# Two-layer convolution kernel: the sums of points 3 and 4 by accumulating DMA, the group norms' steps issued singly, and new instruction lists

## The chip, the cores and the metric

One Trainium2 chip, one core. The metric is device time in microseconds of one execution of the whole program; lower is better. PE is TensorE (matrix products), DVE is VectorE, ACT is ScalarE, POOL is GpSimd, SP is SyncE. SP and POOL do nothing here but issue DMAs, apart from POOL's preparations at the start. SBUF is the working memory, PSUM the memory that PE writes.

## The reference

The input is 16 images of 128 channels and 64x64 pixels, float32. Two residual layers follow each other, each behind a group norm with 32 groups of 4 channels.

```python
def _gn(v, G=32, eps=1e-5):
    g = v.reshape(B_, G, C_ // G, H_, W_)
    m = jnp.mean(g, axis=(2, 3, 4), keepdims=True)
    s = jnp.var(g, axis=(2, 3, 4), keepdims=True)
    return ((g - m) / jnp.sqrt(s + eps)).reshape(v.shape)

# layer 0: a 3x3 convolution as an analog crossbar would compute it
v = jnp.round(jnp.clip(x, -1.0, 1.0) * 127) / 127 * 0.6
fv = patches + 0.1 * patches ** 3              # patches: 3x3 windows of v, zeros around
g = g_pos - g_neg                              # 3 slices of 128x128x3x3
outs = [jnp.einsum('bctfyx,ocyx->btfo', fv, g[i]) for i in range(3)]
adc = lambda y: jnp.clip(jnp.round(y * 0.01 * 256) / 256, -16, 16)
mem_out = adc(outs[2]) + 4 * adc(outs[0]) + 2 * adc(outs[1]) + adc(outs[2])
x = x + mem_out * output_factor + bias

# layer 1: on tokens t = 4096 pixels, 128 -> 64 -> 128 channels
q, k, v = Wq @ xf, Wk @ xf, Wv @ xf
out = Wm @ (q * (exp(B) @ (exp(k) * v)) / (exp(B) @ exp(k)))
x = x + out
```

## The kernel before

**The convolution by points.** Rows are taken in 16 tiles of four. For each tile the kernel does not form the nine shifted products but evaluates the input at six points (0 to 5: the points 0, 1, -1, 2, -2 and infinity of a polynomial in the row), multiplies there with weights evaluated at the same points, and interpolates the four output rows back. Along a row, even and odd columns are combined into sums `cs`, differences `cq` and neighbour differences `cd`, so that a point's product is four matrix products with 512 columns. `weights` (from L286) evaluates the weights once at the start: `us[i]` holds four points of slice `i`, `ud[i]` points 0 and 5.

A *block* is one slice of weights for one image, so an image has three blocks. A block has two *halves*: `h = 0` handles points 1 and 2, `h = 1` points 3 and 4. Half `k` of an image (k = 0 to 5; block k // 2, half k % 2) is made of these operations, whose names stand in the lists below with `.k` behind:

- `q1u`, `q2u`, `q0u`, `q3u` (PE, u = 0 or 1 for the two points): the four products, into the PSUM tiles `pa` and `pb`. `m1u`, `sdu`, `sAu` (ACT) copy `pa` out between them, to `d`, negated to `pb`, and to `s`. A product that reads or continues what a copy needs waits for the copy.
- `Bo` (DVE, L588) makes the second column of the two points' results, in `s[:, :, 1]`; `df` (DVE, L589) takes the difference of the two points into `d`; `sm` (L593 on) puts their sum into `s[:, 1]`. Of the two halves, `h = 0` gets its sum by a DMA that POOL issues and that adds in flight (L597), and `h = 1` by a custom DVE operation that also doubles it (`doubled_sum`, L561).
- Half k of the next block carries the rest of the block before it: `ma` and `mc` (DVE, `middle`, L558: the two inner rows, bounded and rounded to int16; `ma` from the differences, `mc` from the sums of both halves), `S0` and `S3` (DVE, L615 and L618: sums and differences of both halves joined), `P`, `o0`, `o1` (PE: points 0 and 5), `bc` (ACT), `tk` (DVE: the two outer rows), and `aA`, `aB` (adding the block to the image's total: by POOL's DMA or, for the first slice, a doubling on DVE).

**The rest of an image.** `li`, `lj` load a quarter of the next image twice (SP), `sx` and `sy` sum and square it (ACT), `x0`, `xa`, `pmx`, `xb`, `pvx`, `xc`, `xl`, `xd` are its group norm: `x0` a shift, `xa` to `xd` groups of two to five DVE instructions on 128x1 or 128x2 values, `pm` and `pv` two matmuls, `xl` two ACT instructions. Then `n`, `cl`, `s`, `va` quantize, clip and cube it, and `gr`, `er`, `p0`, `p5`, `pa`, `pb`, `cs`, `cq`, `cd`, `e0`, `e5` (DVE) evaluate it at the points. After the convolution `cx` (ACT), `cd0x` to `cd3x` (POOL's accumulating DMA) and `sq` form the layer's output and its squares, `y0` to `yd` are the second group norm, and the second layer runs on four quarters or *pairs* p: `xn`, `kp`, `vp`, `qp`, `ek`, `ekv`, `dn`, `g`, `u`, `ln`, `ex`, `oa`, `ob`, `oc`, `op`, `r`, `rd` (POOL's accumulating DMA), `st` (SP's store).

**What sets the order.** Every engine executes its instructions in the order in which the program names them. That order is written out in lists of operation names. `ORDER` (L39) is one turn of the steady state, which runs for most images; `+1` behind a name means that in this turn the operation belongs to the image before. `FIRST` (L62) is the start with the first images, where `+2` is preparation: `hs`, `hq`, `hn`, `hc`, `hr`, `hv` stand for the sums, squares, quantization, clip, square and value of the four quarters of image 0, `hz`, `hcs`, `hcq`, `hcd` for its points 1 and 2, and `W0a` to `W2p` for steps of the three slices' weights (`a` negates the loaded weights on ACT, `A` is POOL's DMA that adds the positive ones). `LAST` (L95) is the end; there the last block's rest is `tma`, `tmc`, `tS0`, `tS1`, `tk0`, `tk3`, `tx` (joining into the output), `ts` (squares), its norm is `tsh` to `tnd`, and the last image's pairs are written with a capital (`Xn0`, `Kp0`). A wait is inserted wherever an operation needs what another engine or a DMA makes or still reads. A DMA is issued when its turn comes in the queue of the engine that issues it and its inputs are there.

Of the kernel before, what the change touches and what calls it, by code (L numbers as in the profile page):

```python
# [11 lines left out]
I32 = mybir.dt.int32  # L12
# [3 lines left out]
ALU = mybir.AluOpType  # L16
# [23 lines left out]
    cl0+1 q01.2+1 S3.2+1 q00.2+1 sq2+1 tk.2+1 cl1+1 cd0x+1 sA1.2+1 q31.2+1 q11.3+1 s0+1 sA0.2+1  # L40
    m11.3+1 va0+1 q30.2+1 s1+1 q21.3+1 q10.3+1 sq1+1 m10.3+1 P.3+1 q20.3+1 Bo.2+1 sd1.3+1 q01.3+1
    va1+1 df.2+1 lj2+1 sq3+1 lj3+1 gr0+1 sd0.3+1 st3+1 sq0+1 q31.3+1 q30.3+1 sA1.3+1 bc.3+1 q00.3+1
    ya+1 Bo.3+1 sA0.3+1 pmy+1 yb+1 o0.3+1 n2+1 pvy+1 er0+1 st2+1 n3+1 yc+1 o1.3+1 q10.4+1 yl+1 cl2+1
    yd+1 xn0+1 q11.4+1 sm.2+1 tk.3+1 df.3+1 kp0+1 cp+1 vp0+1 m11.4+1 P.4+1 cl3+1 ma.4+1 m10.4+1
    aB.3+1 q20.4+1 ek0+1 bc.4+1 s3+1 ekv0+1 sd0.4+1 dn0+1 sm.3+1 mc.4+1 va3+1 q21.4+1 s2+1 g0+1 li0
    sx0 xn1+1 li1 S0.4+1 u0+1 ln0+1 sd1.4+1 oa0+1 x0 o0.4+1 o1.4+1 q30.4+1 ex0+1 tk.4+1 vp1+1 ob0+1
    qp0+1 kp1+1 oc0+1 aA.2+1 op0+1 va2+1 ek1+1 r0+1 ekv1+1 gr1+1 q01.4+1 sx1 q31.4+1 q00.4+1 sA0.4+1
    P.5+1 S3.4+1 sA1.4+1 bc.5+1 q10.5+1 Bo.4+1 q11.5+1 rd0+1 df.4+1 m10.5+1 er1+1 dn1+1 sy0 g1+1
    u1+1 sm.4+1 o0.5+1 o1.5+1 oa1+1 m11.5+1 st0+1 q21.5+1 aA.4+1 ln1+1 q20.5+1 pa0+1 tk.5+1 ex1+1
    sd1.5+1 pb0+1 q01.5+1 ob1+1 sd0.5+1 q00.5+1 cq0+1 xn2 qp1+1 q30.5+1 q31.5+1 oc1+1 cd0+1 cs0+1  # L50
    Bo.5+1 op1+1 sA0.5+1 kp2 r1+1 li2 vp2 q10.0 ek2 sA1.5+1 P.0 bc.0 q11.0 ekv2 pa1+1 o0.0 m11.0
    m10.0 dn2 q21.0 df.5+1 q20.0 sm.5+1 sx2 o1.0 rd1+1 aB.5+1 sd1.0 pb1+1 mc.0 g2 S0.0 sd0.0 sy2 sy1
    ma.0 q01.0 u2 st1+1 oa2 q30.0 q31.0 ln2 tk.0 ex2 xn3 ob2 q00.0 li3 qp2 kp3 cq1+1 lj0 ek3 sA0.0
    oc2 cs1+1 op2 S3.0 vp3 Bo.0 sA1.0 q11.1 r2 P.1 bc.1 ekv3 df.0 dn3 o1.1 g3 aA.0 cd1+1 m11.1 rd2
    o0.1 sx3 u3 tk.1 q21.1 oa3 sy3 ln3 ex3 q10.1 sd1.1 qp3 m10.1 q20.1 ob3 sd0.1 oc3 op3 p5 sm.0 r3
    q01.1 aB.1 xa q00.1 pmx sA1.1 e5 p0 q30.1 xb sA0.1 e0 cx2 q31.1 cx1 pvx xc Bo.1 lj1 xl rd3 P.2
    bc.2 cx0 cd2x q10.2 q11.2 cd1x o1.2 m11.2 q21.2 df.1 sm.1 cx3 m10.2 xd q20.2 ma.2 o0.2 n0 cd3x
    sd1.2 mc.2 sd0.2 y0 S0.2 n1
# [4 lines left out]
    hs0+2 hs2+2 x0+2 hs3+2 hq0+2 hq2+2 hi+2 hq1+2 hs1+2 hq3+2 xa+2 pmx+2 xb+2 pvx+2 xc+2 xl+2 xd+2  # L63
    hn3+2 hn2+2 hc2+2 hn1+2 hn0+2 W2a+2 W1a+2 W0a+2 hc0+2 hc3+2 hc1+2 W0A+2 hr1+2 hr0+2 hv1+2 hv0+2
    gr0+2 W1A+2 er0+2 hr2+2 W0b+2 li0+1 hv2+2 W0j+2 cp+2 W0c+2 W0f+2 W0e+2 W0d+2 W0g+2 W0i+2 W0h+2
    hr3+2 li1+1 W0J+2 W0n+2 hv3+2 W0l+2 er1+2 sx0+1 W0m+2 W1c+2 x0+1 hz1+2 gr1+2 hcq1+2 W1b+2 pa1+2
    hcs1+2 hcd1+2 W2A+2 W1j+2 sx1+1 W0p+2 sy0+1 W0o+2 q10.0+1 sy1+1 li3+1 hz0+2 li2+1 W1e+2 W2b+2
    hcs0+2 W2c+2 m10.0+1 p0+1 sx3+1 pb1+2 q11.0+1 sx2+1 m11.0+1 q20.0+1 hcq0+2 W1f+2 q21.0+1 sy2+1
    cd1+2 sy3+1 hcd0+2 W1J+2 sd0.0+1 xa+1 sd1.0+1 q01.0+1 sA1.0+1 W1d+2 cs1+2 pmx+1 lj0+1 W2J+2
    q31.0+1 cq1+2 q00.0+1 q30.0+1 xb+1 pvx+1 q11.1+1 W1g+2 sA0.0+1 W1h+2 e0+1 Bo.0+1 m11.1+1 q10.1+1  # L70
    m10.1+1 W2d+2 W1i+2 W2e+2 q20.1+1 W1l+2 lj1+1 xc+1 W1m+2 W2g+2 sd0.1+1 df.0+1 q21.1+1 W2j+2 xl+1
    W0k+2 P.2+1 sm.0+1 sd1.1+1 q00.1+1 xd+1 W1n+2 q01.1+1 W1o+2 W2f+2 bc.2+1 sA0.1+1 p5+1 W2h+2
    q31.1+1 n0+1 q10.2+1 W1p+2 q30.1+1 sA1.1+1 W2i+2 cl0+1 Bo.1+1 m10.2+1 q20.2+1 W2m+2 sd0.2+1 n1+1
    o0.2+1 q11.2+1 W1k+2 q00.2+1 m11.2+1 df.1+1 sm.1+1 q30.2+1 q21.2+1 e5+1 ma.2+1 mc.2+1 S0.2+1
# [886 lines left out]
```

## Time and profile before

| | us |
|---|---|
| median of three runs | 1575.94 (1574.69 to 1576.45) |
| the profiled execution | 1571.91 |
| its span, first to last instruction | 1570.1 |
| mean granted PE clock over the span | 0.979 of full speed |

A line of a group or of the timeline gives: start (timeline only), duration, engine, line of the code, operation, tile written <- tiles read, shape, count; behind it in brackets the engine's idle time before it and who ended that. The DMA lines that matter here:

```profile
acc<-y POOLq DMA_DIRECT2D x62, 512.0 KB, 7.0
x<-in_x_dram POOLq DMA_DIRECT2D x60, 512.0 KB, 8.3
xn<-x POOLq DMA_DIRECT2D x58, 512.0 KB, 4.6
out_dram<-xn SPq DMA_DIRECT2D x58, 512.0 KB, 5.3
s<-s POOLq DMA_DIRECT2D x48, 512.0 KB, 5.6
```

The last number is the median time from issue to landing. `s<-s` is the sum `sm` of the halves `h = 0`, one for each of 48 blocks. In the 92 us of a steady image the DMA engines are busy 66% of the time.

### The profile page before, as it was taken

Reading aid. Unit: us, or ns where it says so; the run is one execution under the profiler, and the core shown is the slowest. Engines: PE = TensorE matmul, PEld = TensorE weight load, DVE = VectorE, ACT = ScalarE, POOL = GpSimd, SP = SyncE. Lnnn points to the kernel's source line nnn. Section 1 sums busy time; section 2 is a strip of 40 time slices with the busy share of each in tenths; the row PEclk is TensorE's granted clock in tenths of the full one; section 3 lists DMA queues with packets and bytes.
Section 4 is the critical chain, followed back from the end, with each engine's and each line's share of the span. In section 5 each row is a group of like instructions: output and inputs, shape, how many; then the busy total and the mean of one; then the engine's idle time right before and its main releaser. Section 6 shows DMA issues by size and latency. Waiting matters only on the chain.

```text
span 1570.1 us, 14797 instructions
## 1 busy us (share of the span) xinstructions
PE 1481.1 (94%) x4684; PEld 564.2 (36%) x4684; DVE 1427.7 (91%) x1817; ACT 1115.6 (71%) x1859; POOL 223.1 (14%) x254
## 2 busy tenths in 40 slices
PE   1589999999999999999999999999999999999996
PEld 0233333333333433333343333433333333333331
DVE  4999999999999999999999999999999999998774
ACT  4655868687686868768686776968678686865654
POOL 2001011120201112011121201112020111201120
PEclk6799999999999999999999999999999999999997
DMA  6226478484756848476593847759385774835375
GB/s 175 78 70 132 111 165 195 107 183 134 153 147 153 209 90 181 138 155 161 131 208 98 174 137 164 173 115 219 96 168 141 165 183 108 195 87 121 81 128 154
DMA packets 67359, 227.01 MB, mean 145 GB/s; under 512 B 7632, under 2 KB 8272, under 8 KB 67280
## 3 DMA queue, kind: packets, MB, share of 16 engines
q0 software_dynamic: 38480, 125.52, 43.2%
q1 hardware_dynamic: 28512, 99.50, 18.4%
q10 hardware_dynamic: 288, 1.05, 0.2%
q8 instruction: 37, 0.61, 0.2%
q14 instruction: 42, 0.34, 0.1%
HBM read 102.30 MB, written 33.55 MB: 87 GB/s over the span
## 4 chain that ended last, share of the span: by engine, by line
PE 51%; DVE 28%; ACT 10%; issue 6%; DMA 5%; DVEq 0%; POOL 0%; ACTq 0%; POOLq 0%
PE py L551 15%; PE pa L551 14%; PE pb L551 7%; PE pz L745 5%; DVE y L558 5%; PE py L767 4%; DVE d L589 3%; DVE acc L558 3%; ACT gs L359 3%; PE py L745 3%; DVE s L615 3%; PE pz L755 2%; DMA x<-in_x_dram 2%; DVE f L502 2%; DVE s L561 2%
## 5 line engine op out<-in xcount | busy, mean ns | idle before, releaser
L551 PE MATMUL py<-v,ud 128*128 128x512 f32 x760 | 363.1, 610 | 0.0
L551 PE MATMUL pa<-cs,us 128*128 128x512 f32 x384 | 195.1, 611 | 34.2 <-DVE us L327 33.1
L551 PE MATMUL pb<-cd,us 128*128 128x512 f32 x384 | 192.7, 609 | 12.4 <-ACT pb L582 10.5
L551 PE MATMUL pa<-cq,us 128*128 128x512 f32 x384 | 197.1, 616 | 4.1 <-ACT d L580 3.9
L551 PEld LDWEIGHTS py<-v,ud 128*128 128x128 f32 x760 | 137.5, 189 | 170.4 <-issue 149.3
L551 PE MATMUL pa<-cd,us 128*128 128x512 f32 x384 | 194.6, 609 | 3.6 <-DVE x L363 2.5
L582 ACT ACTIVATE pb<-pa 128x512 f32<-128x512 f32 x192 | 112.4, 585 | 66.6 <-PE pa L551 61.6
L580 ACT ACTIVATE d<-pa 128x512 f32<-128x512 f32 x192 | 110.8, 594 | 44.1 <-PE pa L551 31.0
L808 POOL DMA_DIRECT2D xn<-x x58 | 50.2, 870 | 607.5 <-ACT xn L778 600.3
L585 ACT ACTIVATE s<-pa 128x512 f32<-128x512 f32 x192 | 111.0, 594 | 35.6 <-PE pa L551 29.8
L588 DVE SCALAR_TENSOR_TENSOR s<-d,pb 128x1024 f32<-128x1024 f32 x96 | 116.6, 1215 | 5.7 <-PE pb L551 5.6
L589 DVE TENSOR_TENSOR d<-s 128x1024 f32<-128x1024 f32 x96 | 117.1, 1220 | 2.9
L551 PEld LDWEIGHTS pa<-cs,us 128*128 128x128 f32 x384 | 68.3, 190 | 140.0 <-issue 53.4
L745 PE MATMUL pz<-xn,w 128*64 128x512 f32 x464 | 117.0, 604 | 0.0
L778 ACT ACTIVATE xn<-py,scalars 128x512 f32<-128x512 f32 x116 | 73.7, 690 | 59.9 <-PE py L767 59.9
L551 PEld LDWEIGHTS pb<-cd,us 128*128 128x128 f32 x384 | 68.3, 190 | 112.0 <-issue 71.0
L640 POOL DMA_DIRECT2D acc<-y x62 | 72.6, 1170 | 250.8 <-DVE y L558 221.1
L551 PEld LDWEIGHTS pa<-cd,us 128*128 128x128 f32 x384 | 67.9, 190 | 110.6 <-issue 71.5
L551 PEld LDWEIGHTS pa<-cq,us 128*128 128x128 f32 x384 | 66.1, 189 | 111.5 <-issue 57.8
L796 ACT ACTIVATE ek<-pz 128x512 f32<-128x512 f32 x60 | 35.8, 597 | 98.5 <-PE pz L745 86.3
L551 PE MATMUL py<-sv,ud 128*128 128x512 f32 x192 | 100.7, 607 | 1.8 <-DVE acc L558 1.6
L597 POOL DMA_DIRECT2D s<-s x48 | 41.0, 855 | 335.4 <-DVE d L589 199.9
(230 smaller groups left out, 2585.0 us busy)
## 6 DMA issues: line engine op xcount, KB each, us to landing
xc<-in_x_dram SPq DMA_DIRECT2D x121, 512.0 KB, 4.8
acc<-y POOLq DMA_DIRECT2D x62, 512.0 KB, 7.0
x<-in_x_dram POOLq DMA_DIRECT2D x60, 512.0 KB, 8.3
xn<-x POOLq DMA_DIRECT2D x58, 512.0 KB, 4.6
out_dram<-xn SPq DMA_DIRECT2D x58, 512.0 KB, 5.3
s<-s POOLq DMA_DIRECT2D x48, 512.0 KB, 5.6
gmat<-in_x_dram POOLq DMA_DIRECT2D x4, 512.0 KB, 7.0
x<-in_g_neg_dram SPq DMA_DIRECT2D x2, 576.0 KB, 11.4
```

Source lines behind the costliest of these rows:

```text
L551: pe.matmul(o if len(r.shape) == 2 else o.rearrange("p (t w) -> p t w", w=W2), w, r, start=start, stop=stop, skip_group_check=True,)
L558: dve._custom_dve(TENSOR_ADD_SAT, out=o, in0=a, in1=b, s0=QMAX, s1=-QMAX)
L580: f"m1{u}.{k}": lambda u=u, a=a: act.activation(d[:, u], a, AF.Copy),
L582: f"sd{u}.{k}": lambda a=a, b=b: act.activation(b, a, AF.Copy, scale=-1.0),
L585: f"sA{u}.{k}": lambda u=u, a=a: act.activation(s[:, u, 0], a, AF.Copy),
L588: f"Bo.{k}": lambda: dve.scalar_tensor_tensor(s[:, :, 1], d, 2.0, pb, ALU.mult, ALU.add),
L589: f"df.{k}": lambda: dve.tensor_tensor(d, s[:, 1], s[:, 0], ALU.subtract),
L640: pool.dma_start(a, y, accum_op=ALU.add)
L745: pe.matmul(self.tiles(o)[h * IC : (h + 1) * IC], w, x[:, t[0] : t[1] : t[2]], start=True, stop=True)
L767: pe.matmul(self.op[h], wm[r, :], self.o[r, :], start=True, stop=True)
L778: act.activation(g[:, t], self.tiles(self.op[h]), AF.Identity, bias=bias_sb)
L808: "rd": lambda: pool.dma_start(self.r, self.x2, accum_op=ALU.add),
```

## The change

Three things. First, the sums of points 3 and 4 (`h = 1`) are made like those of points 1 and 2, by POOL's accumulating DMA. [...]

Second, the groups of small DVE instructions in the norms (`shift`, `begin`, `squares`, `guess`, `finish`) become lists of single operations, so that the order's lists can place each step by itself: `xa` becomes `xa0` to `xa3`, `ya` becomes `ya0` to `ya4`, and so on. In `begin` the mean that the matmul needs is made ahead of the two steps for the variance.

Third, the three lists are written anew. Each engine issues the same operations in another order; the diff shows a few stretches.

```diff
-                "g": lambda: copy(r[:, 0], g1, AF.Copy, scale=1.0 / 6.0),
-                "h": lambda: stt(u[:, 2, 0:3], r[:, 2], 1.0 / 12.0, r[:, 0], ALU.mult, ALU.add),
-                "i": lambda: stt(u[:, 3, 0:3], r[:, 2], 1.0 / 12.0, r[:, 0], ALU.mult, ALU.subtract),
+                "g": lambda: copy(r[:, 0], g1, AF.Copy, scale=1.0 / 3.0),
+                "h": lambda: stt(u[:, 2, 0:3], r[:, 2], 1.0 / 6.0, r[:, 0], ALU.mult, ALU.add),
+                "i": lambda: stt(u[:, 3, 0:3], r[:, 2], 1.0 / 6.0, r[:, 0], ALU.mult, ALU.subtract),
...
         def begin(self):
-            tot, d, self.neg, mean = self.sm(2), self.sm(), self.sm(), self.mean
-            dve.tensor_reduce(tot, self.sums, AX.X, ALU.add)
...
-            dve.scalar_tensor_tensor(d, self.sh, 1.0 / UNIT, mean, ALU.mult, ALU.add)
-            dve.scalar_tensor_tensor(self.neg, d, d, tot[:, 1:2], ALU.mult, ALU.subtract)
-            if self.add is not None:
-                self.all = self.sm()
-                dve.tensor_tensor(self.all, mean, self.add, ALU.add)
...
+            if self.add is not None:
+                steps.append(lambda: dve.tensor_tensor(self.all, mean, self.add, ALU.add))
+            return steps + [
+                lambda: dve.scalar_tensor_tensor(d, self.sh, 1.0 / UNIT, mean, ALU.mult, ALU.add),
+                lambda: dve.scalar_tensor_tensor(self.neg, d, d, tot[:, 1:2], ALU.mult, ALU.subtract),
+            ]
...
         def operations(self, k):
-            return {
-                f"{k}0": self.shift, f"{k}a": self.begin, f"pm{k}": self.means, f"{k}b": self.squares,
-                f"pv{k}": self.variances, f"{k}c": self.guess, f"{k}l": self.root, f"{k}d": self.finish,
-            }
+            o = {f"pm{k}": self.means, f"pv{k}": self.variances, f"{k}l": self.root}
+            for e, steps in zip("0abcd", (self.shift, self.begin, self.squares, self.guess, self.finish)):
+                o |= {f"{k}{e}{n}": f for n, f in enumerate(steps())}
+            return o
...
-    def doubled_sum(o, a, b):
-        dve._custom_dve(TENSOR_TENSOR_REDUCE_ADD_ADD, out=o, in0=a, in1=b, s0=0.0, s1=2.0)
+    def half_difference(o, a, b):
+        dve._custom_dve(TENSOR_TENSOR_REDUCE_SUB_MAX, out=o, in0=a, in1=b, s0=0.0, s1=0.5)
...
-        def sum(self, s, h):
+        def sum(self, s):
+            pool.dma_start(s[:, 1], s[:, 0], accum_op=ALU.add)
+
+        def difference(self, s, h):
+            d = self.d[h]
             if h:
-                doubled_sum(s[:, 1], s[:, 1], s[:, 0])
+                half_difference(d, s[:, 1], s[:, 0])
             else:
-                pool.dma_start(s[:, 1], s[:, 0], accum_op=ALU.add)
+                dve.tensor_tensor(d, s[:, 1], s[:, 0], ALU.subtract)
```

The lists, where the prediction goes through them. In `ORDER`, around `sm.3`, the pair 0 with its `ln0`, and `sm.5`:

```diff
-    yd+1 xn0+1 q11.4+1 sm.2+1 tk.3+1 df.3+1 kp0+1 cp+1 vp0+1 m11.4+1 P.4+1 cl3+1 ma.4+1 m10.4+1
-    aB.3+1 q20.4+1 ek0+1 bc.4+1 s3+1 ekv0+1 sd0.4+1 dn0+1 sm.3+1 mc.4+1 va3+1 q21.4+1 s2+1 g0+1 li0
-    sx0 xn1+1 li1 S0.4+1 u0+1 ln0+1 sd1.4+1 oa0+1 x0 o0.4+1 o1.4+1 q30.4+1 ex0+1 tk.4+1 vp1+1 ob0+1
...
-    Bo.5+1 op1+1 sA0.5+1 kp2 r1+1 li2 vp2 q10.0 ek2 sA1.5+1 P.0 bc.0 q11.0 ekv2 pa1+1 o0.0 m11.0
-    m10.0 dn2 q21.0 df.5+1 q20.0 sm.5+1 sx2 o1.0 rd1+1 aB.5+1 sd1.0 pb1+1 mc.0 g2 S0.0 sd0.0 sy2 sy1
-    ma.0 q01.0 u2 st1+1 oa2 q30.0 q31.0 ln2 tk.0 ex2 xn3 ob2 q00.0 li3 qp2 kp3 cq1+1 lj0 ek3 sA0.0
+    q11.4+1 yc0+1 o1.3+1 st2+1 yc1+1 sm.2+1 yc2+1 yl+1 Bo.3+1 yd0+1 lj3+1 yd1+1 q10.4+1 df.3+1 xn0+1
+    kp0+1 tk.3+1 ma.4+1 m10.4+1 cl2+1 sm.3+1 li0 vp0+1 ek0+1 ekv0+1 aA.2+1 q20.4+1 m11.4+1 n3+1
+    er0+1 cl3+1 sd0.4+1 P.4+1 q21.4+1 dn0+1 sd1.4+1 bc.4+1 S3.4+1 s2+1 g0+1 cp+1 mc.4+1 u0+1 aA.4+1
+    q31.4+1 ln0+1 va2+1 q00.4+1 xn1+1 o1.4+1 S0.4+1 o0.4+1 oa0+1 tk.4+1 q01.4+1 sx0 ex0+1 ob0+1
...
+    aB.5+1 sm.4+1 kp2 cs0+1 q11.0 q10.0 r1+1 ek2 sx2 Bo.5+1 df.5+1 rd1+1 ekv2 sm.5+1 m11.0 m10.0
+    ma.0 dn2 sy1 S3.0 st1+1 li3 q20.0 cd0+1 pa1+1 g2 P.0 bc.0 q21.0 sd1.0 o1.0 u2 sd0.0 ln2 q31.0
+    ex2 mc.0 q00.0 o0.0 oa2 sy2 xn3 sA0.0 sx3 q30.0 S0.0 ob2 tk.0 vp3 qp2 kp3 sy3 pb1+1 oc2 op2
```

In `FIRST`, from the beginning past the first convolution product `q10.0+1`:

```diff
-    hs0+2 hs2+2 x0+2 hs3+2 hq0+2 hq2+2 hi+2 hq1+2 hs1+2 hq3+2 xa+2 pmx+2 xb+2 pvx+2 xc+2 xl+2 xd+2
-    hn3+2 hn2+2 hc2+2 hn1+2 hn0+2 W2a+2 W1a+2 W0a+2 hc0+2 hc3+2 hc1+2 W0A+2 hr1+2 hr0+2 hv1+2 hv0+2
-    gr0+2 W1A+2 er0+2 hr2+2 W0b+2 li0+1 hv2+2 W0j+2 cp+2 W0c+2 W0f+2 W0e+2 W0d+2 W0g+2 W0i+2 W0h+2
-    hr3+2 li1+1 W0J+2 W0n+2 hv3+2 W0l+2 er1+2 sx0+1 W0m+2 W1c+2 x0+1 hz1+2 gr1+2 hcq1+2 W1b+2 pa1+2
-    hcs1+2 hcd1+2 W2A+2 W1j+2 sx1+1 W0p+2 sy0+1 W0o+2 q10.0+1 sy1+1 li3+1 hz0+2 li2+1 W1e+2 W2b+2
+    hs0+2 x00+2 hs1+2 hq1+2 hs3+2 hq2+2 hq0+2 hq3+2 hs2+2 hi+2 xa0+2 xa1+2 pmx+2 xa2+2 xb0+2 xb1+2
+    xa3+2 xb2+2 pvx+2 xc0+2 xc1+2 xc2+2 xl+2 xd0+2 xd1+2 hn0+2 hn1+2 hc1+2 hc0+2 hr1+2 hr0+2 hn2+2
+    hv1+2 hn3+2 hv0+2 er0+2 gr0+2 hc2+2 W0a+2 W0A+2 cp+2 hc3+2 hr3+2 hv3+2 hr2+2 ho+2 hv2+2 W1a+2
+    li0+1 er1+2 W2a+2 W0b+2 gr1+2 p0+1 pa1+2 W2A+2 W0J+2 pb1+2 e0+1 W0c+2 W0e+2 W1A+2 W0d+2 sx0+1
+    W0f+2 cs1+2 W0g+2 W0j+2 x00+1 W0i+2 W0h+2 hz1+2 W0m+2 W2c+2 W0l+2 sy0+1 hcs1+2 W2j+2 W0o+2 W0n+2
+    hcq1+2 li1+1 q10.0+1 W1c+2 W2b+2 W1b+2 m10.0+1 W0p+2 li2+1 sx1+1 W2d+2 hz0+2 sy1+1 sx2+1 W1d+2
+    hcs0+2 hcq0+2 W1e+2 hcd0+2 W1f+2 P.2+1 hcd1+2 q11.0+1 W1g+2 W2f+2 q20.0+1 sy2+1 m11.0+1 sd0.0+1
```

In `LAST`, the last half's sum and the rest of the last block:

```diff
-    ex3+0 Bo.5+1 q01.5+1 tP1+0 sm.4+1 qp3+0 tp1+0 ob3+0 Lx2+0 sA1.5+1 df.5+1 sm.5+1 oc3+0 tma+0
-    tS1+0 op3+0 tmc+0 tS0+0 tx1+0 tp0+0 r3+0 tk3+0 tx2+0 tsh+0 tP0+0 to0+0 ts1+0 to1+0 tx3+0 tk0+0
+    oa3+0 q31.5+1 u3+0 q30.5+1 q01.5+1 r2+0 sA1.5+1 ln3+0 ex3+0 Lx3+0 tP1+0 Bo.5+1 qp3+0 df.5+1
+    Lc2+0 ob3+0 Lx1+0 sm.4+1 oc3+0 tp0+0 sm.5+1 op3+0 tma+0 tS1+0 r3+0 tmc+0 tp1+0 tk3+0 tP0+0 to1+0
```

## The prediction

> **What bounds the kernel now.** I read the busy times first, then the span by stages, then TensorE's own timeline inside one image, then the start by engine, then the DMAs.
>
> ```profile
> PE 1481.1 (94%) x4684; PEld 564.2 (36%) x4684; DVE 1427.7 (91%) x1817; ACT 1115.6 (71%) x1859; POOL 223.1 (14%) x254
> ```
> ```profile
> 30.00:61.60 31.60, 6.84 (x8) 2.15 (x9) 29.76 (x35) 18.44 (x41) 0.31 (x1) 0.55 0.43 106
> 61.60:110.70 49.10, 44.78 (x99) 18.63 (x100) 48.04 (x68) 31.08 (x55) 1.68 (x2) 0.97 0.29 77
> 110.70:203.21 92.51, 88.62 (x243) 35.51 (x242) 88.93 (x108) 63.00 (x110) 12.72 (x14) 1.00 0.53 121
> ...
> 759.19:851.50 92.31, 91.39 (x293) 34.84 (x293) 87.04 (x111) 69.14 (x116) 13.57 (x15) 1.00 0.66 154
> ...
> 1221.41:1315.12 93.71, 91.65 (x293) 34.78 (x293) 87.11 (x111) 69.15 (x116) 13.58 (x15) 1.00 0.66 152
> ```
> ```profile
> 1201.89 3.67 PE L551 MATMUL py<-v,ud 128*128 128x512 f32 x8
> 1206.32 1.12 PE L551 MATMUL pb<-cd,us 128*128 128x512 f32 x2 [0.76 <-ACT pb L582]
> ```
>
> Columns of the stage rows: stretch, length, busy time of PE, weight load, DVE, ACT, POOL, then PE clock, DMA share, GB/s. The averages (PE 94%, DVE 91%) hide three regimes. From 30 to 62 us DVE is busy 29.8 of 31.6 us and PE nearly idle: the start is **DVE's**. From 204 to 1407 us, 13 images, an image takes 92.3 to 93.7 us (1204.3/13 = 92.64) with PE busy 91.4 to 91.7: the middle is **PE's**, and DVE, at 87.1, is next. The only regular PE wait there is the 0.76 us of the last fence. From 1530 us the tail is a chain of latencies. So an image cannot take less than about 92.31 - 0.76 = 91.55 us in this instruction set, and all that the middle can give is 13 x (92.64 - 91.55) = 14 us.
>
> The start:
>
> ```profile
> 11.31 0.14 DVE L352 TENSOR_SCALAR x<-x 128x1 f32<-128x1 f32 x1
> ...
> 28.36 2.43 DVE L470 SCALAR_TENSOR_TENSOR f<-f,n 128x1056 f32<-128x1056 f32 x2 [2.88 <-ACT f L464]
> ```
> ```profile
> 11.49 1.15 ACT L359 ACTIVATE gs<-xc,x 128x1024 int16<-128x1024 f32 x1 [9.41 <-DVE x L352]
> ...
> 24.10 2.20 ACT L308 ACTIVATE x<-x 128x1152 f32<-128x1152 f32 x2
> 26.21 1.15 ACT L308 ACTIVATE s<-s 128x1152 f32<-128x1152 f32 x1
> 27.26 2.04 ACT L464 ACTIVATE f<-n 128x1056 f32<-128x1056 int16 x2
> ```
> ```profile
> 51.95 2.08 PE L551 MATMUL pa<-cs,us 128*128 128x512 f32 x2 [33.09 <-DVE us L327]
> ...
> 61.62 2.04 PE L551 MATMUL pa<-cd,us 128*128 128x512 f32 x2 [2.54 <-DVE x L363]
> ```
>
> ACT's first square waits until 11.49 because the shift `x0` (L352) stands on DVE behind a sum over a chunk that lands at 10.2. Three weight negations (L308, 3.3 us) stand on ACT ahead of the first squares (L464) that DVE needs at 28.36. TensorE gets its first convolution product at 51.95 and the first `cd` product at 61.62.
>
> **The change, part by part.**
>
> *Doubled sums.* L561 (48 times, 1227 ns) goes; POOL issues 48 more adds like these:
>
> ```profile
> L561 DVE CUSTOM_DVE_ANT_0 s<-s 128x1024 f32<-128x1024 f32 x48 | 58.9, 1227 | 1.1
> L597 POOL DMA_DIRECT2D s<-s x48 | 41.0, 855 | 335.4 <-DVE d L589 199.9 <-ACT gs L359 112.2 <-PE pa L551 10.4
> ```
>
> DVE loses 3 x 1.23 = 3.7 of its 87.1 us an image. The difference of half 1 becomes a custom operation; the trace lacks it. Bounds: 1.22 us (L589) to 1.23 us (L561, same inputs and shape), and at the far end 2.28 us (L511, twice the elements), which would hand 3 x 1.06 of the 3.7 us back. I take 1.23. The weights' factors are scales of instructions that stay: nothing.
>
> The cost is latency. The 48 existing adds landed 4.5 to 9.8 us after issue, median 5.6, nine in ten under 6.5. What waits for a sum is `mc` (custom add, L558) and then `S0` (L615); behind them on DVE stand `tk` and the attention pairs' steps. For the tightest, `sm.5`, DVE has from the issue to `mc.0`: `ekv2` 0.69, `ma.0` 1.36, `S3.0` 1.22, `cd0` 2.28, `pa1` 1.25, `u2` 0.69 = 7.5 us. After it `mc.0`, `oa2`, `S0.0`, `ob2`, `tk.0`, `oc2` take 1.36 + 0.69 + 1.22 + 0.69 + 1.30 + 0.69 = 5.95, while PE has 6.4 us up to `op2`, which needs `oc2`. So PE feels `sm.5` only if it lands later than about 7.5 + 0.5 = 8 us after issue. For `sm.3` the same sum (`tk.3`, `ma.4`, `cl2`, `ekv0`, `er0`, `cl3`, `S3.4`) is 6.6 us. For `sm.1` DVE has only 4.4 us of work, but PE has 7.0 us up to the same place, and DVE follows PE there. At the median all three are covered, from DVE's 92.4 - 83.4 = 9 us of slack an image.
>
> POOL: 13.6 + 3 x 0.86 = 16.2 of 92 us. The queue: a transfer of 512 KB on it costs 43.2% x 1570 / 244 = 2.8 us of all sixteen engines, so the DMA share goes from 0.66 to 0.66 + 8.4/92 = 0.75.
>
> [...] In the trace POOL's issues take 0.85 us in most groups and 1.17 in `acc<-y`. [...]
>
> *Small steps one by one.* The count stays. A dependent 128x1 step takes 0.19 us start to start (16.78, 16.97, 17.16), one with other work behind it 0.07 (11.31 to 11.37). With some 24 steps an image the bounds are 0 and 24 x 0.12 = 2.9 us of DVE; I take half, and again only DVE gains. Where latency counts, in the last norm, `neg` moves behind the matmul: -0.3 us.
>
> *Order: PE.* I counted in both steady lists where TensorE goes between 128x128 products and the narrower ones of the pairs: 26 changes before, 26 after, and 4 norm matmuls in each. The same products and changes give the same PE work, so 91.55 stays the floor. The wait of 0.76 us is that of `q30.4` for the copy `sd1.4`. Its chain:
>
> ```profile
> 1199.62 1.24 DVE L561 CUSTOM_DVE_ANT_0 s<-s 128x1024 f32<-128x1024 f32 x1
> ...
> 1204.44 0.68 DVE L800 TENSOR_TENSOR ek<-gs,pz 128x512 f32<-128x512 f32 x1
> ```
> ```profile
> 1205.15 0.63 ACT L801 ACTIVATE ek<-ek 128x512 f32<-128x512 f32 x1 [0.21 <-DVE ek L800]
> 1205.69 0.58 ACT L582 ACTIVATE pb<-pa 128x512 f32<-128x512 f32 x1
> ```
>
> The sum `sm.3` ends on DVE 3.6 us before `u0` (L800) starts, in the same queue, `ln0` (L801) waits for `u0`, and the copy stands behind `ln0` on ACT. The sum leaves DVE, and the new list has `sd1.4` ahead of `ln0`: this wait goes twice over. Other pairs get tighter (`q10.0` to `q20.0`: 1.2 us of PE work against 4.4 of ACT, before 5.6 against 3.0). Bounds for the middle: -14 us (all waits gone) and +14 (one more wait like this one per image, 13 x 1.09). I take -4: its wait gone, half of that spent on new ones.
>
> *Order: the start.* `x00` follows `hs0` directly, so squares start at 7.1; the last chunks land at 10.15 and 10.79, the fourth square ends at about 10.2 + 3 x 1.27 = 14.0, before 16.56: -2.5. After the norm, ACT now does one quantization, then the squares, and the negations come later. From the norm's end to the end of `er0`/`gr0` DVE has `hn1` 1.0, `hc1`, `hc0` 0.8, a wait of 0.7, `hv1`, `hv0` 2.4, `er0`, `gr0` 3.1 = 8.0 us; before, 20.4 to 33.9 = 13.5. So -8.0 at that point. From there to the first product DVE has 18.5 us of instructions (`gr1`, `p0`, `pa1`, `pb1`, `e0`, `cs1` are ahead now) and I add 1.3 for waits: 25.9 + 19.8 = 45.7 against 51.95. The first `cd` product (`hcd1`) comes 7.8 us of DVE work later, at 53.5 against 61.62. But `cd1` and `cq1` (2.28 + 1.22), done by 65 before, are still to do: -4.6 to -8.1. Up to 203 us PE then idled 4.3 + 3.9 = 8.2 us beside a full DVE, of which the missing sums can give some 2 back. I take **-7** for the start (bounds -12 and -3).
>
> *Order: the tail.* Before, from the end of the last `df.5` (1517.7) DVE runs 14.2 us without a gap to `tx0`. They are 1.2 for the sum, 3.1 for `oc3`, `tma`, `tS1`, and 9.9 from `tmc` on. Now `tmc` waits for `sm.5`, 5.6 us after its issue, with `ob3` (0.6, ahead of `df.5` before) and the 3.1 us to fill it: -0.6 + 5.6 + 9.9 = 14.9, so +0.7, and at 9.8 us of landing +5. The last four pairs are reshuffled, which I can't size: ±2. With the norm's -0.3 I take **0** (bounds -2 and +5).
>
> Sum: -7 - 4 + 0 = -11 us on the profiled execution's 1571.91 (span 1570.1). The runs' median is 1575.94, 4 us above it; the same -11 gives **1565**.
>
> **Rivals.**
> 1. *Only the start pays.* The middle gets as many waits as it loses: 1575.94 - 7 = 1569. For it: PE's work is the same and its margins are as many and as tight as before. Against: DVE's 5 us of relief loosens them.
> 2. *The start's lead is eaten.* PE is the bound from 62 us on and takes up a lead only if DVE keeps it; if `cd1` and `cq1` and a late add cost what was gained: 1575, no change.
> 3. *Slower: the sums land late.* `aB.5`, `sm.4`, `rd1` and `sm.5` stand within 3 us on POOL's queue, beside `li3` on SP's. Four reads issued within 5.3 us in the trace landed 6.3, 8.7, 8.6 and 11.9 us after issue. If `sm.5` lands at 9.8, past the 8 us where it decides, PE loses 1.8 us an image; `sm.3`, at 9.8 against 6.6 less 1 us of slack, 1 more. That is 14 x 1.8 to 14 x 2.8 = 25 to 39, less the start's 7: about 1600. Against: three of the 48 adds took over 8 us, and what `aB.5` and `sm.4` wait for (`tk.5`, `df.4`) is done 7 to 8 us of PE work earlier.
> 4. *The halved difference is slow* (2.28 us): DVE back at 86.6, new waits of DVE for nothing: 1572.
>
> **Chances.** Forecast 0.50 (1565, own range 1555 to 1570), only the start 0.16, eaten 0.11, late sums 0.20, slow custom operation 0.03. Anything within 0.2%, 3 us, counts as no change: faster 0.67, same 0.11, slower 0.22. Range 1554 to 1586: down to most of the middle's 14, up to where one of the late sums costs half its price.
>
> **What would show it.** First convolution product near 46 us and first `cd` product near 54; DVE at 83 us or less per image and PE still at 91.4; the image's period near 92.2; no DVE wait on `s<-s` over 2 us; DMA share 0.75. A period over 93 with DVE's custom add waiting for `s<-s` would make rival 3 right and this wrong; a first product after 50 us would take the start away.

## The result, and the profile after

The changed kernel takes **1583.37 us** (median of five runs, 1582.6 to 1588.26) against 1574.69 for the kernel before on the same chip: ratio **1.0059**, 95% interval 1.0046 to 1.0071. It is slower by 9 us where 11 us less was forecast. Its profiled execution took 1583.88 us, with a span of 1582.2 at a granted PE clock of 0.982.

To see where the time went, I cut both spans at the end of the sixth `Bo` of each image (DVE, `Bo.5`), an operation that both lists have; images count from 0:

| stage | before, us | after, us | difference | forecast |
|---|---|---|---|---|
| start, up to `Bo.5` of image 2 | 305.92 | 295.02 | -10.9 | -7 |
| 13 images, up to `Bo.5` of image 15 | 1210.01 | 1233.21 | **+23.2** | -4 |
| tail | 54.21 | 53.93 | -0.3 | 0 |
| span | 1570.1 | 1582.2 | +12.1 | -11 |

The mark in image 2 stands some 2 us of PE's work earlier in the changed kernel (after 676 matrix products instead of 680). PE's idle time up to it fell from 56.3 to 47.2 us, so the start gained about 9 us and the middle lost about 21. The start and the tail did what was forecast. The middle lost 1.8 us an image. The busy times by engine, and one image of the middle as a row of stages (columns as in the rows of before):

```profile
PE 1485.1 (94%) x4684; PEld 562.8 (36%) x4684; DVE 1380.7 (87%) x1769; ACT 1117.1 (71%) x1859; POOL 263.9 (17%) x302
```
```profile
672.33:766.67 94.34, 91.86 (x296) 34.84 (x292) 84.34 (x108) 69.24 (x115) 16.12 (x18) 1.00 0.74 167
```

PE has the same work and 2.4 us of it idle. DVE has been relieved (87 to 84.3 us an image), so it is not the bound. The start, in PE's timeline and ACT's:

```profile
46.68 2.08 PE L564 MATMUL pa<-cs,us 128*128 128x512 f32 x2 [30.34 <-DVE us L334]
...
56.50 1.02 PE L564 MATMUL pb<-cd,us 128*128 128x512 f32 x2
57.36 1.96 PE L564 MATMUL pa<-cd,us 128*128 128x512 f32 x4
```
```profile
7.19 1.15 ACT L369 ACTIVATE gs<-xc,x 128x1024 int16<-128x1024 f32 x1 [5.10 <-DVE x L359]
```

What PE waits for in the middle (us in total, times, longest), 295 to 1400 us. Before, the one large entry was 8.4 us for the copy `pb` (the 0.76 us of `q30.4`):

```profile
PE pz L388 <- DVE y L381: 11.8, 11, 1.5
PE pa L564 <- ACT d L593: 7.8, 12, 1.9
PE pa L564 <- ACT s L598: 4.4, 10, 1.3
PE pb L564 <- ACT pb L595: 2.9, 9, 0.7
```

The old wait is gone and four new ones, 27 us together in these eleven to twelve images, stand between 45 and 57 us of every image. `pz L388` is the second norm's first matmul (`pmy`); DVE's step L381 ahead of it needs the squares `sq` (ACT, L369), and a square needs its input add `cd0x` to `cd3x` (POOL, L714). One image, PE, ACT and POOL in turn:

```profile
717.73 1.12 PE L564 MATMUL pa<-cs,us 128*128 128x512 f32 x2 [0.33 <-ACT s L598]
...
720.64 1.13 PE L564 MATMUL pa<-cq,us 128*128 128x512 f32 x2 [0.93 <-ACT d L593]
...
728.50 0.38 PE L388 MATMUL pz<-y,grp 128*128 128x1 f32 x2 [1.02 <-DVE y L381]
```
```profile
718.87 1.15 ACT L369 ACTIVATE gs<-x,y 128x1024 int16<-128x1024 f32 x1 [1.19 <-DMA x<-in_x_dram]
...
722.83 1.15 ACT L369 ACTIVATE gs<-x,y 128x1024 int16<-128x1024 f32 x1 [0.44 <-DMA x<-in_x_dram]
...
726.63 1.15 ACT L369 ACTIVATE gs<-x,y 128x1024 int16<-128x1024 f32 x1 [1.60 <-DMA x<-in_x_dram]
```
```profile
704.57 0.86 POOL L714 DMA_DIRECT2D x<-in_x_dram  x1 [0.84 <-ACT x L711]
708.93 0.84 POOL L607 DMA_DIRECT2D s<-s  x1 [3.50 <-DVE x L406]
710.02 2.61 POOL L714 DMA_DIRECT2D x<-in_x_dram  x3 [0.25 <-ACT x L411]
```

Read from the bottom: POOL stands 3.5 us in front of the new add `sm.1` (L607; it must not overwrite what the difference on DVE still reads). Behind it wait three input adds, headed by `cd3x`, whose copies ended at 706.0, 707.6 and 709.7. They go out together at 710 and land at 718.8, 722.7 and 726.5; three squares wait for them, with the copies that PE needs behind them on ACT; and PE waits last. `cd3x` could not have gone before 709.7 in any case: that it heads the three holds back the two that were ready.

### The profile page after: what moved, and what is told of

It is laid out like the page before. It is cut to its first block, busy times and chain, and to the rows that moved or that the text cites. A ratio compares the mean times of both kernels' runs of the same rounds, so it can differ in the third digit from the quotient of the medians.

```text
span 1582.2 us, 14962 instructions
## 1 busy us (share of the span) xinstructions
PE 1485.1 (94%) x4684; PEld 562.8 (36%) x4684; DVE 1380.7 (87%) x1769; ACT 1117.1 (71%) x1859; POOL 263.9 (17%) x302
## 3 DMA queue, kind: packets, MB, share of 16 engines
q10 hardware_dynamic: 288, 1.05, 0.2%
## 4 chain that ended last, share of the span: by engine, by line
PE 62%; DMA 16%; ACT 7%; DVE 7%; issue 6%; POOL 2%; DVEq 0%; ACTq 0%; SPq 0%; POOLq 0%
PE pa L564 20%; PE py L564 18%; DMA x<-in_x_dram 13%; PE pz L762 6%; PE pb L564 5%; PE pz L772 4%; PE py L784 4%; PE py L762 3%; ACT x L711 3%; DMA acc<-y 1%; POOL x L714 1%; ACT d L593 1%; DMA s<-s 1%; DVE y L571 1%; ACT gs L369 1%
## 5 line engine op out<-in xcount | busy, mean ns | idle before, releaser
L564 PE MATMUL pa<-cs,us 128*128 128x512 f32 x384 | 201.6, 616 | 39.8 <-DVE us L334 30.3
L564 PE MATMUL pa<-cq,us 128*128 128x512 f32 x384 | 201.1, 615 | 9.9 <-ACT d L593 9.6
L564 PE MATMUL pb<-cd,us 128*128 128x512 f32 x384 | 200.6, 614 | 3.6 <-ACT pb L595 3.2
L564 PE MATMUL pa<-cd,us 128*128 128x512 f32 x384 | 199.1, 607 | 0.6 <-ACT pb L595 0.4
L607 POOL DMA_DIRECT2D s<-s x96 | 88.1, 918 | 502.6 <-DVE d L614 214.4
L657 POOL DMA_DIRECT2D acc<-y x62 | 63.3, 1022 | 376.8 <-DVE y L571 301.2
L369 ACT ACTIVATE gs<-x,y 128x1024 int16<-128x1024 f32 x60 | 68.7, 1145 | 41.8 <-DMA x<-in_x_dram 41.6
```

The source lines that it names most:

```text
L369: act.activation(o, a, AF.Square, bias=self.sh, scale=UNIT, accum_out=self.sums[:, 1, q : q + 1])
L564: pe.matmul(o if len(r.shape) == 2 else o.rearrange("p (t w) -> p t w", w=W2), w, r, start=start, stop=stop, skip_group_check=True,)
L607: pool.dma_start(s[:, 1], s[:, 0], accum_op=ALU.add)
L657: pool.dma_start(a, y, accum_op=ALU.add)
```

## The experiments

Two measures serve all of them: when each add lands, and the period of an image. Landings are medians over nine images, in us after `Bo.5` of the image before; the period is the mean of images 3 to 12.

| run | input adds issued | `sm.1` issued, landed | input adds landed | period |
|---|---|---|---|---|
| before | 31.7 32.9 36.5 37.0 | on DVE | 38.3 41.4 45.0 48.9 | 92.55 |
| after | 32.3 37.7 38.2 38.8 | 36.6, 41.9 | 39.4 46.2 50.2 **54.1** | 94.36 |
| e3 adds first | 32.3 34.0 35.6 37.7 | 38.2, **52.5** | 39.5 42.0 44.9 48.7 | 104.46 |
| e11 second add ahead | 32.3 34.0 37.2 37.7 | 36.6, **45.3** | 39.6 42.2 49.2 53.0 | 96.91 |
| e5 `sm.1` on DVE | 32.3 37.7 38.3 38.8 | on DVE | 39.4 44.0 48.5 **52.5** | 92.54 |
| e6 both | 32.3 34.0 35.6 37.7 | on DVE | 39.5 42.1 45.4 49.4 | **91.18** |

All edits of lists are in `ORDER`, the steady part, unless told otherwise. Ratios are to the kernel before, with the 95% interval.

### e1 to e4: traffic, order, or the queue

**e1**, all sums of half 1 on DVE again, everything else as changed:

```diff
-        def sum(self, s):
-            pool.dma_start(s[:, 1], s[:, 0], accum_op=ALU.add)
+        def sum(self, s, h):
+            if h:
+                doubled_sum(s[:, 1], s[:, 1], s[:, 0])
+            else:
+                pool.dma_start(s[:, 1], s[:, 0], accum_op=ALU.add)
```

> The changed kernel with its order, start and tail, but the sums of half 1 on DVE again (doubled, with the weights of before). Theory T (traffic: the three more adds an image are what makes the input adds cd0x to cd3x land late, so that the squares and the second norm are late): the median landing of x<-in_x_dram falls from 10.2 us to 9 or less, the squares' waits on ACT from 36 us to under 15, the period from 94.3 to 92.5 us, the time to 1583 - 13 x 1.8 = about 1560. Rival O (order: the input adds stand too close to each other and to the loads and stores in the new list, whoever does the sums): landing 9.5 to 10.5, period 94 or more, since DVE has 3.7 us an image more as well: 1580 to 1600.

Measured: 1586.30, 1.0082 (1.0067 to 1.0097). Traffic alone is out: without one added transfer the new order is as slow. But the time is lost elsewhere in part. The small waits at 45 to 52 us are gone, the norm's matmul waits 7.6 us in 11 images instead of 11.8, and two new waits stand where DVE's sum `sm.5` delays the pairs (0.8 and 0.2 us, seen again in e10). The input adds still land at 53.3, because `cd3x` at their head waits for the last copy (e10 takes it from there, and they land at 50.5, and the wait at the norm's matmul is gone). In e1, e7 and e10 the first input add is issued 1.1 to 1.4 us later after the mark than in the other runs of the new list, so their landings are to be read as that much earlier.

**e2**, the sums alone in the old order (the edit of e1 the other way round, in the kernel before, with `half_difference` and the weights' factors):

> The kernel before with its own order, start and tail, and only the sums of half 1 by accumulating DMA (halved difference, weights doubled). Theory T (traffic): the landing of x<-in_x_dram rises from 8.3 to 9.5 us or more, the period by 1 us or more: 1588 or slower, since the start's gain isn't in it. Rival O (order): the landing stays under 9, the period at 92 to 93; 1570 to 1580. The prediction's third rival, in its own place (DVE's custom add waits for the sums), would show here as waits of DVE on s<-s of over 1 us an image and 1590 to 1600, because this order gives the sums no time to land.

Measured: 1811.69, 1.1508 (1.1458 to 1.1557). This is the third rival in its own place, at many times its price. `sm.1` lands 9.2 us after issue and `x<-in_x_dram` after 10.5; DVE's custom adds wait 138 us for `s<-s` in 11 images. Giving the sums to DMA is not a change that an order made for DVE survives.

**e3**, each input add behind its own copy, so `sm.1` comes last (the squares, further down in the list, follow in the order of landing):

```diff
-    P.2+1 xc0+1 q11.2+1 m10.2+1 cd0x+1 df.1+1 cx2+1 bc.2+1 m11.2+1 cx3+1 q20.2+1 xc1+1 sm.1+1 xc2+1
+    P.2+1 xc0+1 q11.2+1 m10.2+1 cd0x+1 cd1x+1 df.1+1 cx2+1 cd2x+1 bc.2+1 m11.2+1 cx3+1 cd3x+1 q20.2+1
+    xc1+1 sm.1+1 xc2+1
```

> The changed kernel with one edit of its steady order: each input add goes out right behind the copy that it adds to, so cd1x, cd2x, cd3x are ahead of sm.1 on POOL's queue, and the squares follow in the order of landing. Theory Q (queue: sm.1 waits on POOL for the difference on DVE, 3.5 us in the trace, with three input adds behind it that have been ready): the last input add lands 2 to 4 us sooner, the squares' waits fall from 36 us to under 12, PE's wait on the norm's matmul from 11.8 to under 5, period 93, time 1566 to 1572; sm.1 lands later and mc.2 may wait up to 2 us for it on DVE, which has slack. If the lateness has another cause, the period stays at 94 and the time at 1580 or more.

Measured: **1719.97**, 1.0934 (1.0916 to 1.0953), a complete miss, and the run that taught most. The input adds land where expected (48.7), and the squares' and norm's waits are gone from PE. But `sm.1`, in line behind four adds, lands 10.6 us later than in the changed kernel, and `mc.2` has no slack for it. DVE's and PE's timelines of one image:

```profile
786.43 1.29 DVE L571 CUSTOM_DVE_ANT_0 acc<-s,s 128x1024 int16<-128x1024 f32 x1 [10.98 <-DMA s<-s]
```
```profile
789.72 2.08 PE L564 MATMUL pa<-cs,us 128*128 128x512 f32 x2 [10.72 <-ACT s L598]
```

The wait passes on whole: custom add, `S0`, the copy `s`, PE. I had assumed 2 us of wait at most, covered by DVE's idle time; idle time elsewhere in the image does not help the instruction that is next.

**e4**, one store taken out of the bunch (`st2` moved to the head of the turn):

```diff
-    P.2+1 xc0+1
+    st2+1 P.2+1 xc0+1
...
-    q11.4+1 yc0+1 o1.3+1 st2+1 yc1+1
+    q11.4+1 yc0+1 o1.3+1 yc1+1
```

> The changed kernel with one edit of its steady order: the store st2 stands at the head of the turn, so that SP issues it some 8 us sooner, outside the bunch of adds, loads and stores. Theory T (traffic of any kind in the bunch): a transfer of 512 KB is 2.8 us of all sixteen engines, so the input adds issued last land 1 to 2.8 us sooner, the squares' waits fall by a third to two thirds, the time by 13 x 0.5 to 13 x 1.5: 1564 to 1577. If only the adds on POOL's own queue count (theory Q), nothing changes: 1581 to 1586.

Measured: 1579.99, 1.0042 (1.0026 to 1.0059), between the two ranges. The store goes out 17 us sooner; the last input add lands 0.2 us sooner, the period falls by 0.1 us. This store is not what holds the adds back. A second store and two loads of SP's queue stay beside them, and the sixteen DMA engines stay full there (busy share 1.05 over 12 us of the bunch, 1.03 in the changed kernel), so what SP's traffic as a whole adds to their spacing is open.

### e5 to e8: the two places on the queue

**e5**, only `sm.1` on DVE (`i == 0`, with the old factors for that slice), in a hole of 1.1 us that DVE had there:

```diff
-    m11.2+1 cx3+1 q20.2+1 xc1+1 sm.1+1 xc2+1 xl+1 xd0+1
+    m11.2+1 cx3+1 q20.2+1 xc1+1 xc2+1 xl+1 sm.1+1 xd0+1
...
+            if h and self.i == 0:
+                doubled_sum(s[:, 1], s[:, 1], s[:, 0])
```

> The changed kernel with one of its three new adds undone: sm.1 is a doubled sum on DVE again (1.23 us, put where DVE waits 1.1 us for the root of the input's norm), with the weights of the first product as before; sm.3 and sm.5 stay on the queue, the order of the input adds is the changed one (cd3x at their head). Theory P (sm.1 and the head cd3x both hold back input adds that are ready; in the last run without sums on DMA the adds still landed at 53.3 us of the image, against 54.1): the last input add lands 0.8 to 2 us sooner, PE's waits fall from 2.4 to about 1.5 us an image: 1566 to 1576. Theory T (each transfer in the bunch delays the last one by its 3.8 us): the last lands 3.5 us sooner, the waits go, the period is 92.0: 1552 to 1560. If neither, 1580 or more.

Measured: 1556.80, 0.9887 (0.9871 to 0.9904). The last add lands 1.6 us sooner, as theory P had it, but the time falls as theory T had it: P allowed only for the wait at the norm, and the small waits in front of it were the same lateness (e8). PE's waits fall from 2.40 to 1.06 us an image and its busy time by 0.5. The norm's wait is what remains, 9.9 us in 11 images.

**e6**, e5 with the input adds first, as in e3:

> As the kernel with sm.1 on DVE, and the input adds each right behind the copy that they add to (as in the run that took 1720 us, where sm.1 was the last of the queue and landed at 52.5 us of the image instead of 41.9). Both theories: nothing waits for sm.1 any more, the input adds land at 48 us or sooner instead of 54, the waits of the squares and of PE's norm matmul go, the period is 91.9 to 92.3: 1550 to 1560. If the time stays above 1570, the lateness of the input adds is not what costs the middle its time.

Measured: **1542.01**, 0.9795 (0.9778 to 0.9811), the best of all and below what was expected. POOL's timeline and the row of one image:

```profile
687.27 0.85 POOL L720 DMA_DIRECT2D x<-in_x_dram  x1 [0.80 <-ACT x L717]
689.01 0.86 POOL L720 DMA_DIRECT2D x<-in_x_dram  x1 [0.89 <-ACT x L717]
690.63 0.84 POOL L720 DMA_DIRECT2D x<-in_x_dram  x1 [0.76 <-ACT x L717]
692.75 0.85 POOL L720 DMA_DIRECT2D x<-in_x_dram  x1 [1.28 <-ACT x L411]
```
```profile
655.07:746.16 91.09, 91.07 (x296) 34.91 (x292) 85.25 (x108) 69.13 (x115) 15.21 (x17) 1.00 0.73 168
```

Each add leaves when its copy is done. PE is busy 91.07 of 91.09 us, without one wait of over 0.1 us from image 3 to 12. DVE works 0.9 us an image more than in the changed kernel, which costs nothing.

**e7**, the mirror image (`i > 0` in place of `i == 0`: `sm.3`, `sm.5` on DVE, `sm.1` by DMA):

> The mirror image: sm.3 and sm.5 on DVE, only sm.1 by DMA, all else as changed. They stand 12 and 40 us away from the input adds, so if the bunch around sm.1 is the cause, the input adds land as before (54 us of the image), PE's waits at 45 to 57 us stay, and DVE has 2.5 us more: 1580 to 1590. If the number of adds as such is the cause, 1560 to 1572.

Measured: 1607.93, 1.0211 (1.0192 to 1.0230). The input adds land as late as ever (55.1) and the wait at the norm is whole; what I missed is that `sm.5` on DVE makes PE wait as well (the third line; e10 shows how), and the start is 4 us longer. PE's waits, 299 to 1354 us:

```profile
PE pz L388 <- DVE y L381: 11.4, 11, 1.1
PE pa L564 <- ACT d L596: 9.3, 11, 1.4
PE pz L768 <- ACT xn L815: 9.0, 11, 0.8
```

**e8**, `sq0` and `sq3` exchanged:

> The changed kernel with two names exchanged in its steady order: sq0, whose add has landed at 39.4, goes first on ACT, and sq3 takes its place, so ACT no longer stands 1.2 us before its first square with the copies for PE behind it. Theory of one deficit (PE's three small waits at 45 to 52 us and the one of 1.03 at 56 are the same lateness of the last input add, split up): the small waits shrink, the wait at 56 us grows by as much, the time stays within 3 us of 1583. If the waits are separate, 13 x 0.7 to 13 x 1.2 less: 1567 to 1575.

Measured: 1585.83, 1.0067 (1.0045 to 1.0088). PE's waits, 294 to 1333 us:

```profile
PE pb L564 <- ACT pb L595: 11.9, 10, 2.5
PE pz L388 <- DVE y L381: 11.3, 10, 2.0
PE pa L564 <- ACT s L598: 3.3, 8, 0.7
```

The wait for `d` is gone and the one for `pb` has grown. All waits together are 2.44 us an image (images 3 to 12), against 2.40 in the changed kernel. It is one deficit, which a change of places only splits up differently.

### e9 to e12: the other parts

**e9**, e6 with the norms' steps in groups again (`xa0 xa1 xa2 xa3` and so on, each at its first step's place):

> The kernel with sm.1 on DVE and the input adds first (1542 us, PE without a wait in the middle), with the norms' small steps in the steady order put together again, each group at the place of its first step. The prediction had this part at 0 to 2.9 us of DVE an image and nothing for PE. If that is right, DVE's busy time changes by under 3 us an image and the time by less than 4: 1538 to 1546. If the steps one by one carry the gain of the middle (large DVE work filling the waits between the steps), the time rises by 13 x 0.5 or more: over 1549.

Measured: 1542.98, 0.9801 (0.9786 to 0.9815). The steps one by one are worth nothing: in the steady list DVE's busy time differs by 4.9 us over 16 images, 0.3 an image, and PE does not feel it.

**e10**, e6 with all three sums on DVE:

> The input adds first, and all three sums of half 1 on DVE as before the change: the order's part alone, with the queue mended. The run with all sums on DVE and the adds late had PE waits of 1.0 us at 13.3 and 0.2 at 72.4 us of the image, which have nothing to do with the input adds; its 0.65 at the norm's matmul should go. So the period is 92.2 to 92.5, the time 1555 to 1562, and the two remaining adds by DMA (sm.3, sm.5) are worth the 13 to 20 us to 1542. If it reaches 1545, moving sums to DMA is worth nothing at all; over 1570 the input adds were not what held this order back.

Measured: 1568.62, 0.9965 (0.9948 to 0.9982). The two adds that stay on the queue in e6 are worth 27 us. DVE's and PE's timelines show it for `sm.5`:

```profile
576.67 1.22 DVE L574 CUSTOM_DVE_ANT_0 s<-s 128x1024 f32<-128x1024 f32 x1
...
583.85 0.68 DVE L816 TENSOR_TENSOR ek<-gs,pz 128x512 f32<-128x512 f32 x1
```
```profile
588.18 1.08 PE L761 MATMUL pz<-xn,w 128*64 128x512 f32 x4 [0.82 <-ACT xn L808]
```

The sum pushes DVE's `u2` (L816) back, ACT's logarithm and exponential follow it, the scaling `xn3` stands behind them, and PE waits for it. The expectation had these waits (1.25 us an image) but not that PE's busy time would be 0.6 us an image longer and the start 5.6 us.

**e11**, the changed kernel with `cd1x` alone ahead of `sm.1` (squares again in the order of landing):

```diff
-    cd0x+1 df.1+1 cx2+1 bc.2+1 m11.2+1 cx3+1 q20.2+1 xc1+1 sm.1+1 xc2+1
+    cd0x+1 cd1x+1 df.1+1 cx2+1 bc.2+1 m11.2+1 cx3+1 q20.2+1 xc1+1 sm.1+1 cd2x+1 cd3x+1 xc2+1
```

> The changed kernel, all sums by DMA, with cd1x ahead of sm.1 on the queue and cd2x, cd3x behind it (squares in the order of landing). A queue served in order gives sm.1 the second add's 3 to 4 us: it lands at 45 us of the image instead of 41.9, and the last input add stays at 53 to 54, since as many transfers are ahead of it. If mc.2 on DVE has no slack (three adds ahead cost 10.6 us of landing and 10 us of period), the period is 95.5 to 98, the time 1600 to 1630: no place on this queue is early enough for both. If mc.2 has 3 us of slack, 1575 to 1585.

Measured: 1620.31, 1.0294 (1.0278 to 1.0309), as expected of an `mc.2` without slack.

**e12**, e6 with the same edit in `LAST`, for the last two images:

> The kernel of 1542 us with the input adds right behind their copies in the list of the last two images too, and the squares in the order of landing. There the periods were 93.8 and 98.1 us, against 91.1 in the middle; if late input adds are a part of this, it gains 1 to 5 us: 1537 to 1541; if the last images wait for other things, 1541 to 1543.

Measured: 1551.89, 0.9857 (0.9842 to 0.9872), 10 us worse than e6: the mistake of e3 again. In the last image `rd3`, POOL's add for the last pair of the image before, now stands behind two input adds; the copy `cx3`, which overwrites what `rd3` reads, waits for it on ACT, and PE 9.58 us behind that. POOL's and ACT's timelines:

```profile
1422.46 1.19 POOL L831 DMA_DIRECT2D xn<-x  x1
```
```profile
1432.05 1.15 ACT L717 ACTIVATE x<-acc,scalars 128x1024 f32<-128x1024 int16 x1 [9.46 <-DMA xn<-x]
```

## Why the prediction was wrong

**The cause, from the runs.** Two adds on one queue have a time by which they must land. For the last input add: e6 has PE at the norm's matmul at 53.0 us without a wait, and from the landing to that matmul it is 2.0 us (726.54 to 728.50), so the limit is 51.0. The changed kernel is 3.1 us past it and its period 3.18 above e6's; e5 is 1.5 past it and 1.36 above. For `sm.1`: landings of 45.3 (e11) and 52.5 (e3) give PE waits of 3.56 and 11.04 us an image, so its limit is at about 41.5 to 41.7, and the changed kernel lands it at 41.9. Behind that come three input adds, which land 4.3, 4.0 and 3.9 us after one another, where 9.3 us are left for all three. The list met one limit, nearly, at the expense of the other, and none of the orders tried met both with all four input adds and `sm.1` on the queue. Taking `sm.1` off it and putting each input add behind its own copy meets both (e6); without the second step the last add is still 1.5 us late (e5). Not tried was to make the difference `df.1`, which `sm.1` waits for on POOL, earlier on DVE.

**The step that failed** is "Order: PE", with its value of -4 for the middle (bounds ±14; measured +23.2). It asked which waits go and sized the new ones by half the old one (half of 13 x 0.76 us would have been -5; -4 was taken), without a row for it. Measured are new waits of 2.40 us an image against 0.97 before, and 0.4 us more of PE's busy time. It did not follow the sentence on queues in "Doubled sums": there "a transfer of 512 KB on it costs 2.8 us" was turned into a DMA share of 0.75, which came out right (0.74), and not into landings, one after another, of the adds that the new list puts behind `sm.1`. With 2.8 us each the last would even have been in time (41.9 + 3 x 2.8 = 50.3 against 51.0). The spacing to take was in the trace of before: its four input adds, issued within 5.3 us, land 3.1, 3.6 and 3.9 us after one another (row "before" of the table), and the prediction read such rows only for `sm.5` and `sm.3`. And the lists showed `cd0x`, `sm.1`, `cd3x`, `cd1x`, `cd2x` in a row. I asked of each new sum whether it would land in time, and never of the transfers behind it.

**Rival 3** had the mechanism, a queue too full for what waits behind it, and its price of 1.8 us an image happens to equal the measured loss. Its place and its victim were wrong: not the sums of the burst `aB.5`, `sm.4`, `rd1`, `sm.5`, but the input adds behind `sm.1`. Its own sign, DVE waiting over 2 us for `s<-s`, did not appear: the longest such wait of the custom add in the middle was 0.9 us, for `sm.1`. That 1583 lies inside the stated range is luck: its upper end was priced by late sums.

**What held.** *The start*: first product at 46.68 (forecast 45.7), first `cd` product at 56.50 (53.5), about 9 us gained (7, bounds 3 to 12). The lead at the `cd` product was 5.1 us instead of 8.1, and PE's idle time from there to some 200 us fell from 8.2 to 3.8 us instead of by 2: two errors that nearly cancel. *The tail*: -0.3 (0). *The old wait* of `q30.4` went. *The halved difference* takes 1.23 us, as assumed; rival 4 is out. *POOL's issues* of the sums take 0.92 us in the mean against 0.85 before, and 0.87 in e2, which has the same adds in the old order. *The small steps*: 0.3 us an image of DVE, PE nothing (e9). *The floor*: 91.1 us an image in e6, against 91.55. *DVE*: 84.3 us an image, not 83.4. Rivals 1 and 2 had the middle at zero or the lead eaten once; it was eaten twice.

**What the parts are worth.** Four runs with the input adds in the order of the changed list hold each of the two kinds of sums on DVE and on the queue:

| us | `sm.3`, `sm.5` on DVE | `sm.3`, `sm.5` by DMA |
|---|---|---|
| `sm.1` on DVE | 1586.3 (e1) | 1556.8 (e5) |
| `sm.1` by DMA | 1607.9 (e7) | 1583.4 (changed) |

So `sm.1` by DMA costs 22 to 27 us, and `sm.3` and `sm.5` by DMA gain 25 to 30: together they are worth next to nothing. With the input adds behind their copies the pair gains 27 us (e10 to e6). That place of the input adds gains 15 to 18 us where `sm.1` is on DVE (e5 to e6, e1 to e10), and costs 137 where it is on the queue (changed to e3). The start, up to the mark in image 2, is 7 to 15 us shorter than before in all of these but e3.

## What to carry to other kernels

When an operation moves to a DMA queue, ask of it when it lands, and then ask the same of each transfer that is issued after it on that queue; a transfer that must wait for an engine holds back all that are ready behind it (in the changed kernel two input adds whose copies had ended at 706.0 and 707.6 left from 710 on). Compare landing times with the place where the first consumer stands, not with the share of the DMA engines or with idle time somewhere else in the period. And before a whole class of operations is moved, look for the one among them that meets the bunch: here two of three were worth moving, and the third cost as much as they brought.

## What the runs showed of the hardware

**The queue of the adds.** An add of 512 KB from SBUF with no other add in flight lands mostly 4.5 us after its issue (median of 63 in the changed kernel and of 26 before; 4.45 at the least, 6.2 at the most). The five in a row of the changed kernel land 2.5 to 4.3 us after one another, the four of e6 2.7 to 4.0. The changed kernel's DMA adds and does no more (`accum_op=ALU.add`): the factor 2 stands in the weights of points 3 and 4, and their difference is halved on DVE, in 1.23 us. Whether a DMA could scale as well, no run tried. All adds of the changed kernel are in one line of its profile (queue, kind: packets, MB, share of 16 engines):

```profile
q0 software_dynamic: 45392, 150.69, 52.1%
```

Whether `sm.1` could have a queue of its own, no run tried.

**The clock after a long wait of PE.** After the longest wait in the middle of the changed kernel, 1.92 us, a pair of products takes 1.12 us and the granted clock of the next 4.4 us is 1.00. In e11 a wait of 3.92 us is followed by 4.61 us at 0.63, and in e8 one of 2.45 us by 4.60 at 0.63 (the last row):

```profile
730.00:737.40 7.40, 7.40 (x18) 2.97 (x16) 3.67 (x7) 6.59 (x9) 1.60 (x2) 1.00 1.05 211
741.39:746.00 4.61, 4.61 (x7) 1.98 (x8) 4.61 (x6) 2.83 (x6) 0.00 (x0) 0.63 1.02 342
...
1006.68:1011.28 4.60, 4.59 (x9) 2.03 (x9) 0.55 (x4) 3.35 (x5) 0.00 (x0) 0.63 0.80 207
```

If the clock is 1.00 or 0.50 there, about 3.4 us of each of the last two rows are at 0.50 (4.61 x 0.37 / 0.50), an estimate from the rows. PE's busy time is 2.1 us an image longer in e11 than in e6 (93.23 against 91.15), and the granted clock over the span is 0.964 against 0.982; in e2 it is 0.923. What decides whether a wait is followed by half clock, these three examples do not say.

In the middle of the changed kernel the clock costs nothing: it is 1.00 from 56.31 to 1544.52 us. Outside it the traces have stretches at 0.50: of 40.96 us from 15.35 and of 10.24 us from 1544.52 in the changed kernel, of 44.37 us from 13.80, of 3.41 us from 61.59 and of 10.24 us from 1532.73 in the kernel before. Each is 1, 3, 12 or 13 times 3.41 us.

Where PE waits more, its busy time is longer too: 91.15 us an image with no wait (e6), 91.45 with about one (e5), 91.93 with about four (the changed kernel) and 92.35 with six or seven (e7), by an estimate from these some 0.2 us for each. Why is not shown.
